# Products that nothing reads, in the lull slots of a TensorE plan

## The chip, the cores and the metric

The kernel runs on one core of a Trainium2 chip. The metric is device time in microseconds (us) of one launch. TensorE is called PE below, VectorE DVE, ScalarE ACT, GpSimd POOL, and SP issues most of the DMAs.

## The reference

The input is 32 images of 128 channels and 32 x 32 pixels. Four residual layers follow each other, each on a group-normalised copy of its input. The second one fills nearly all of the time.

```
x = x + conv3x3(gn(x))                       # layer 0
x = x + mamba_block(gn(x))                   # layer 1: 4 views of each image, 1024 steps each
x = x + coordinate_attention(gn(x)) * gn(x)  # layer 2: two short mambas over row and column means
x = x + quantum_circuit(gn(x))               # layer 3: a per-pixel map with 4 angles

# one mamba "way" (one view of one image), L = 1024, 256 inner channels, 16 states
h[t] = exp(dt[t] * A[n]) * h[t-1] + dt[t] * u[t] * B[t, n]
y[t] = sum over n of h[t] * C[t, n]  (+ D * u[t]),  then gated, projected, added
```

## The kernel before

**Tiling.** The 256 inner channels are two halves h of 128 partitions, and the 1024 pixels lie along the free axis. One *step* is one half and one state n: 32 steps make a way, four ways an image, and 32 images (and two short ways of the attention) give 4160 steps. `Steps.run` walks them.

**A step on the engines.** For step i ACT computes the decay `da` (L633). PE makes the input `bu` in PSUM (`spread`): in 11 of the 32 steps of a way ("turned" ones) by eight transposes of a tile that ACT has scaled (L647), in the other 21 by two bf16 products of 48 rows that copy B over the partitions (L653), after which DVE multiplies them by `du` in place (`input`, L669). DVE scans (`scan`, L677), POOL multiplies the scan's result `hh` by C (`weigh`, L686), and PE sums it over n into PSUM by eight transposes (`add`, `sum`, L722; for n = 0 there are eight products with the skip weights, L701, and the sum comes one iteration later). `bu` has two buffers, so PE may write step i + 1 when scan i - 1 has ended.

**The order.** Inside `manual_schedule` each engine executes in the order in which Python emits. One iteration i of `Steps.run` emits: the decay of step i + 3, reads of finished products (`flush`), `spread(i + 1)`, `scan(i)`, `input(i + 1)`, then one slot of the plan, `scale(i + 4)`, `weigh(i)`, `add(i - 2)` and the DMA that loads C for step i + 3.

**The plan.** All other work (convolutions, projections, dt, gates, statistics of the neighbouring images and ways) is cut into `Stage` objects with a hand-written cost for (PE, ACT, POOL, DVE). `Plan.slot` takes stages that are due, as long as each engine has credit; a slot is worth `SLOT = 3.3` us, and `load_of(i)` says what the step itself costs on the four engines. Since the streams have fixed windows relative to each way, the slots repeat from image to image: slot s of way q is filled alike in nearly all images. Some slots get no stage that uses PE.

**Products and their readers.** A stage takes one of two PSUM buffers of the pool `psm` by `Kernel.mm`; the instruction that reads it is kept in `waiting` (ACT), `behind` (DVE) or `single` (one half of a pair) and is emitted later by `flush`. `open` counts accumulations that are begun and not ended.

Of the kernel before, what the change touches and what calls it, by code (L numbers as in the profile page):

```python
# [12 lines left out]
F32 = mybir.dt.float32  # L13
# [6 lines left out]
P = 128  # L20
# [3 lines left out]
DS = 16  # L24
# [204 lines left out]
class Stage:  # L229


    def __init__(
        self, run, *, pe=0.0, act=0.0, pool=0.0, dve=0.0, takes=False, gap=1, at=0, when=lambda: True,
        pair=None,
    ):
        self.run, self.cost = run, (pe, act, pool, dve)


        self.takes, self.gap, self.at, self.when, self.pair = takes, gap, at, when, pair
# [257 lines left out]
class Plan:  # L497
# [16 lines left out]
    def slot(self, i, steps):  # L514

        k = self.k
        self.credit = [min(c + self.SLOT - own, self.SLOT) for c, own in zip(self.credit, steps)]

        def slack(s):
            return (s["end"] - i) / sum(stage.gap for stage in s["left"])  # L520

        for s in sorted((s for s in self.streams if s["start"] <= i), key=slack):
            stage = s["left"][0]
            if i < max(stage.at, s["last"] + stage.gap):
                continue
            if stage.takes and k.open > 1 or not stage.when():
                continue
            if stage.takes and self.pair not in (None, stage.pair) and slack(s) > 0.8:
                continue
            if slack(s) > 1.2 and any(c > 0 and c_ <= 0 for c, c_ in zip(stage.cost, self.credit)):  # L530
                continue
            stage.run()
            if stage.pair:
                self.pair = stage.pair if k.open or k.single else None
            self.credit = [c_ - c for c, c_ in zip(stage.cost, self.credit)]
            s["last"] = i
            s["left"].pop(0)
        late = [s for s in self.streams if s["left"] and s["end"] < i]
        assert not late, (i, [(s["start"], s["end"], len(s["left"])) for s in late])
        self.streams = [s for s in self.streams if s["left"]]  # L540

    def alone(self):

        k, i = self.k, 10**6
        while self.streams:
            for s in list(self.streams):
                k.flush(False)
                s["left"].pop(0).run()
                if not s["left"]:
                    self.streams.remove(s)  # L550
            k.flush(False)
        k.flush()


class Steps:
# [11 lines left out]
    def run(self, ways, plan):  # L567

        k = self.k
        steps = [(w, h, n) for w in ways for h in range(2) for n in range(DS)]  # L570
        self.steps = steps
        for i in range(3):
            self.load(i)
        for i in range(3):
            self.decay(i)
        self.spread(0)
        self.input(0)
        for i in range(len(steps) + 2):
            self.evict()
            self.decay(i + 3)  # L580
            k.flush(False, vector=False)
            self.spread(i + 1)
            self.catch_up()
            self.scan(i)
            k.flush(False)
            self.input(i + 1)
            if self.has(i):
                plan.slot(i, self.load_of(i))
            self.scale(i + 4)
            self.weigh(i)  # L590
            self.add(i - 2)
            self.load(i + 3)
        self.evict()
        k.flush()
# [123 lines left out]
    def sum(self, i):  # L718
        k, (w, h, n) = self.k, self.steps[i]
        t = self.hh.pop(i)  # L720
        for g, b, at in self.blocks(w):
            k.nc.tensor.matmul(  # L722
                self.y[g][: w.bl, b], t[:, at], k.ident,
                start=False, stop=(n == DS - 1 and b == w.per - 1), is_transpose=True,
            )
# [17 lines left out]
class Kernel:  # L743
# [21 lines left out]
    def exps(self):  # L765

        if not self.plain:
            self.nc.scalar.preload_act_table_set("natural_log_exp_and_others")  # L768
        self.plain = True

    def later(self, read, more=False, vector=False):

        if vector:
            self.behind.append(read)
        elif more:
            self.single = read
        else:
            self.waiting += [self.single, read] if self.single else [read]
            self.single = None
# [137 lines left out]
    def images(self):  # L917
        tc, nc, d = self.tc, self.nc, self.d
        with ExitStack() as ctx:
# [91 lines left out]
            def way_out(im, w):  # L1011


                def run(c):
                    def run():
                        cs = slice(c * 512, (c + 1) * 512)
                        if w.v == 0 and c == 0:
                            im.o = img.tile([P, HW], F32, tag="tmp", name="o")
                        ps = self.mm()
                        for h in range(2):  # L1020
                            nc.tensor.matmul(
                                ps, m.ow[:, w.v, h], w.sz[:, h, cs], start=(h == 0), stop=(h == 1)
                            )
                        into = im.o[:, cs]
                        had = into if w.v else im.hpad[:, 3 + c * 512 : 3 + (c + 1) * 512]
                        self.later(
                            lambda: nc.vector.scalar_tensor_tensor(
                                into, ps, 0.25, had, ALU.mult, ALU.add
                            ),
                            vector=True,  # L1030
                        )
                    return run

                return [Stage(run(c), pe=1.75, dve=0.7, takes=True, gap=2 - c) for c in range(2)]
# [513 lines left out]
```

## Time and profile before

| | us |
|---|---|
| median of 3 runs | 15073.83 (15066.03 to 15084.82) |
| profiled execution, its own time | 15093.06 |
| its span, first to last instruction | 15091.3 |
| mean granted TensorE clock | 0.920 of full speed |
| DVE busy | 13401.1 (89%) |
| PE busy | 13174.8 (87%) |
| POOL busy | 12747.8 (84%) |
| ACT busy | 12256.2 (81%) |

A busy PE is not a PE at its peak: its clock can be granted at half speed, and the same product then counts twice the time. What an engine waits for, and what ended the wait, stands behind each row of the groups, of the waits and of the timeline.

### The profile page before, as it was taken

How to read it: one execution, taken by the hardware profiler on the slowest of the kernel's cores; microseconds unless marked ns; L12 is line 12 of the kernel's file. 1: busy time of each engine (PE TensorE's matmuls, PEld its weight loads, DVE VectorE, ACT ScalarE, POOL GpSimd, SP SyncE). 2: the span in 40 equal slices, each digit the busy share in tenths (PEclk: the TensorE clock that was granted, in tenths of full speed). 3: DMA queues.
4: the chain of work that ended last, by engine and by line, in shares of the span. 5: the costliest groups of instructions: out<-in, count | busy, mean ns of one | idle time of the engine just before them, and what ended most of it. 6: DMA issues, size and time to landing. Idle time of an engine off the chain costs nothing. (4 is left out here: it accounts for less than half of the span.)

```text
span 15091.3 us, 197699 instructions
## 1 busy us (share of the span) xinstructions
PE 13174.8 (87%) x70318; PEld 8507.7 (56%) x70318; DVE 13401.1 (89%) x8776; ACT 12256.2 (81%) x21181; POOL 12747.8 (84%) x6529
## 2 busy tenths in 40 slices
PE   7888888888888888988888888888888888888876
PEld 4555555555555555555555555555555555555532
DVE  7999989999989999898999999999999999999774
ACT  6888888888888888888888888888888888888642
POOL 6888888888888888888888888888888888888764
PEclk8999999999999999999999999999999999999877
DMA  3444444444444444444444444444444444444431
GB/s 118 159 155 155 156 153 154 156 159 156 155 153 153 158 155 159 154 154 154 153 157 159 154 157 153 155 152 158 157 157 154 155 153 154 157 159 157 144 107 68
DMA packets 633895, 2277.61 MB, mean 151 GB/s; under 512 B 77481, under 2 KB 81145, under 8 KB 632777
## 3 DMA queue, kind: packets, MB, share of 16 engines
q1 hardware_dynamic: 630600, 2263.06, 43.8%
q8 instruction: 554, 9.08, 0.2%
q14 instruction: 437, 3.57, 0.1%
q10 hardware_dynamic: 2304, 1.90, 0.0%
HBM read 2221.35 MB, written 43.33 MB: 150 GB/s over the span
## 5 line engine op out<-in xcount | busy, mean ns | idle before, releaser
L686 POOL TENSOR_TENSOR hh<-hh,cc 128x1024 f32<-128x1024 f32 x4160 | 9771.8, 2366 | 1752.5 <-DVE hh L677 1086.5
L677 DVE TENSOR_TENSOR_SCAN hh<-da,bu 128x1024 f32<-128x1024 f32 x4160 | 9415.4, 2280 | 618.6 <-PE bu L647 234.9
L722 PEld LDWEIGHTS y<-cbig,hh 128*128 128x128 f32 x33280 | 4065.2, 150 | 1793.5 <-issue 1285.2
L722 PE MATMUL y<-cbig,hh 128*128 128x128 f32 x33280 | 4762.6, 290 | 181.8 <-POOL hh L686 181.4
L633 ACT ACTIVATE da<-dt,m_na 128x1024 f32<-128x1024 f32 x4096 | 4607.2, 1144 | 352.8 <-DVE hh L677 344.9
L669 DVE TENSOR_TENSOR bu<-du,bu 128x1024 f32<-128x1024 f32 x2752 | 3336.8, 1213 | 680.5 <-PE bu L653 679.6
L662 ACT ACTIVATE but<-dut,bt 128x128 f32<-128x128 f32 x11264 | 3433.6, 392 | 0.0
L653 PE MATMUL bu<-parts,sel 48*128 48x512 bf16 x5504 | 1761.5, 402 | 638.6 <-DVE hh L677 630.0
L280 PE MATMUL mm<-hpad,m_wc 128*128 128x512 f32 x4096 | 2063.6, 627 | 104.1 <-ACT relu L386 68.6
L647 PE MATMUL bu<-cbig,but 128*128 128x128 f32 x11264 | 1606.7, 290 | 378.1 <-DVE hh L677 331.6
L647 PEld LDWEIGHTS bu<-cbig,but 128*128 128x128 f32 x11264 | 1388.4, 151 | 445.2 <-issue 287.8
L280 PEld LDWEIGHTS mm<-hpad,m_wc 128*128 128x128 f32 x4096 | 710.1, 193 | 908.6 <-issue 753.5
L653 PEld LDWEIGHTS <-sel 48*128 48x128 bf16 x5504 | 322.6, 95 | 1149.9 <-DVE hh L677 687.2
L402 POOL TENSOR_TENSOR w<-w,du 128x1024 f32<-128x1024 f32 x260 | 613.8, 2361 | 38.3 <-ACT w L395 38.3
L299 PE MATMUL mm<-uc,m_xw 128*128 128x512 f32 x1024 | 602.9, 720 | 31.0 <-ACT sz L762 22.6
L701 PEld LDWEIGHTS y<-m_skip,uc 128*128 128x128 f32 x4096 | 554.4, 212 | 132.8 <-issue 79.8
L762 ACT ACT_TABLE_LOAD x483 | 619.7, 1283 | 8.5
L768 ACT ACT_TABLE_LOAD x483 | 619.7, 1283 | 8.5
L439 ACT COPY dut<-mm 128x512 f32<-128x512 f32 x512 | 294.9, 576 | 407.0 <-PE mm L434 406.9
L406 POOL TENSOR_TENSOR dt<-dt,w 128x1024 f32<-128x1024 f32 x260 | 615.3, 2366 | 0.2
L411 POOL TENSOR_TENSOR du<-dt,uc 128x1024 f32<-128x1024 f32 x260 | 614.3, 2363 | 0.2
L406 POOL TENSOR_TENSOR dt<-dt,relu 128x1024 f32<-128x1024 f32 x260 | 613.9, 2361 | 0.0
(219 smaller groups left out, 10394.3 us busy)
## 6 DMA issues: line engine op xcount, KB each, us to landing
cc<-rows SPq DMA_DIRECT2D x4160, 512.0 KB, 3.8
xt<-in_x SPq DMA_DIRECT2D x32, 512.0 KB, 5.9
x<-xt SPq DMA_DIRECT2D x32, 512.0 KB, 3.7
xt<-x SPq DMA_DIRECT2D x32, 512.0 KB, 4.0
out<-xt SPq DMA_DIRECT2D x32, 512.0 KB, 2.9
rows<-dbl SPq DMA_DIRECT2D x130, 64.0 KB, 4.3
stats<-st SPq DMA_DIRECT2D x32, 36.0 KB, 1.5
means<-stats SPq DMA_DIRECT2D x1, 1152.0 KB
```

The lines of the kernel that those rows point to most:

```text
L280: nc.tensor.matmul(self.view(ps), m.wc[:, v, j, h * P : (h + 1) * P], self.taps(j, c), start=(j == 0), stop=(j == 3),)
L406: nc.gpsimd.tensor_tensor(self.dt[h], self.dt[h], t[name], op)
L633: k.nc.scalar.activation(t, w.dt[h], AF.Exp, scale=w.m.na[:, h, n : n + 1])
L647: k.nc.tensor.matmul(t[:, b * P : (b + 1) * P], but[:, b], k.ident, start=True, stop=True, is_transpose=True,)
L653: k.nc.tensor.matmul(t[:, cs], k.sel[:, n], w.parts[:, cs], start=True, stop=True)
L662: k.nc.scalar.activation(t[:, b], w.dut[h][:, b], AF.Copy, scale=w.bt[:, b, n : n + 1])
L669: k.nc.vector.tensor_tensor(t, w.du[h], t, ALU.mult)
L677: k.nc.vector.tensor_tensor_scan(way(t), way(self.da.pop(i)), way(self.bu.pop(i)), 0.0, ALU.mult, ALU.add)
L686: k.nc.gpsimd.tensor_tensor(t, t, self.cc.pop(i), ALU.mult)
L722: k.nc.tensor.matmul(self.y[g][: w.bl, b], t[:, at], k.ident, start=False, stop=(n == DS - 1 and b == w.per - 1), is_transpose=True,)
L762: self.nc.scalar.activation(*args, AF.Silu, **kw)
L768: self.nc.scalar.preload_act_table_set("natural_log_exp_and_others")
```

## The change

`Plan.slot` now returns what is left of the slot by its own costs: SLOT, plus the DVE cost of the stages that it ran, less the PE cost of these stages and of the step. After `add(i - 2)`, `Steps.run` hands this, less 0.8 us, to a new function `Kernel.idle`. That one emits one product per 0.25 us, at most six, and none if there would be fewer than two or if more than one read is outstanding. The products have 48 rows and 512 columns in bf16 (the stationary operand is a piece of the identity, the moving one a piece of the selectors `sel`), all go into one tile `unread` from the pool `psm`, and nothing reads them. In the built program there are 2687 such products in 791 slots: 603 slots with three, 124 with six, 62 with two, two with five. Instructions of the other four engines stand in the same order as before.

```diff
@@ Plan.slot
         self.credit = [min(c + self.SLOT - own, self.SLOT) for c, own in zip(self.credit, steps)]
+        pe = dve = 0.0
...
             self.credit = [c_ - c for c, c_ in zip(stage.cost, self.credit)]
+            pe, dve = pe + stage.cost[0], dve + stage.cost[3]
...
         self.streams = [s for s in self.streams if s["left"]]
+
+        return self.SLOT + dve - pe - steps[0]
@@ Steps.run
-            if self.has(i):
-                plan.slot(i, self.load_of(i))
+            rest = plan.slot(i, self.load_of(i)) if self.has(i) else 0.0
             self.scale(i + 4)
             self.weigh(i)
             self.add(i - 2)
+            k.idle(rest - 0.8)
             self.load(i + 3)
@@ Kernel
+    def idle(self, us):
+
+        n = min(int(us / 0.25), 6)
+        if n < 2 or len(self.waiting) + len(self.behind) + self.open + bool(self.single) > 1:
+            return
+        ps = self.psm.tile([P, 512], F32, tag="mm", name="unread")
+        for _ in range(n):
+            self.nc.tensor.matmul(
+                ps, self.half[: 3 * DS], self.sel[:, :4].rearrange("p n d -> p (n d)"),
+                start=True, stop=True,
+            )
```

## The prediction

> **What bounds the kernel.** I read the page first: its busy row, its clock row, and in the groups what ended DVE's idle time.
>
> ```profile
> PE 13174.8 (87%) x70318; PEld 8507.7 (56%) x70318; DVE 13401.1 (89%) x8776; ACT 12256.2 (81%) x21181; POOL 12747.8 (84%) x6529
> ...
> PEclk8999999999999999999999999999999999999877
> ...
> L677 DVE TENSOR_TENSOR_SCAN hh<-da,bu 128x1024 f32<-128x1024 f32 x4160 | 9415.4, 2280 | 618.6 <-PE bu L647 234.9
> ...
> L669 DVE TENSOR_TENSOR bu<-du,bu 128x1024 f32<-128x1024 f32 x2752 | 3336.8, 1213 | 680.5 <-PE bu L653 679.6
> ```
>
> DVE sets the pace: no engine is busier, and what it waits for is PE, 680 us ahead of L669 and 235 us ahead of L677. These 915 us are all that faster products can win. PE is late for two reasons: heavy slots, and a clock that is now and then at half speed. The mean clock of 0.920 means that 2 x 0.080 x 15091 = 2415 us ran at half. The clock records show 417 such stretches, 2426 us together, most of them 3.41 us long. Between 200 and 14,400 us DVE idles 319 of 2017 us under a slow clock (15.8%), and 1000 of 12,183 us under a fast one (8.2%). If slow time cost what fast time does, 0.076 x 2017 = 153 us would be saved. That bounds the gain loosely from above.
>
> Then I cut a stretch of the second way of an image into 3.41 us windows at the clock's own edges (columns: window, its length, then PE, PEld, DVE, ACT, POOL busy, PEclk, DMA share, GB/s):
>
> ```profile
> 4646.14:4649.56 3.42, 1.49 (x11) 0.91 (x10) 3.29 (x3) 3.42 (x5) 2.42 (x2) 1.00 0.49 157
> 4649.56:4652.97 3.41, 2.88 (x10) 1.65 (x10) 3.38 (x5) 3.19 (x11) 3.38 (x2) 0.50 0.48 157
> ...
> 4690.52:4693.93 3.41, 2.63 (x11) 1.45 (x12) 3.28 (x3) 3.41 (x7) 2.56 (x2) 1.00 0.80 221
> 4693.93:4697.34 3.41, 3.41 (x12) 1.70 (x10) 2.64 (x2) 3.41 (x10) 2.81 (x2) 0.50 0.78 304
> 4697.34:4700.76 3.42, 3.42 (x13) 1.78 (x12) 2.71 (x2) 3.42 (x8) 1.88 (x1) 0.50 0.63 210
> 4700.76:4704.17 3.41, 3.41 (x17) 3.41 (x18) 3.38 (x6) 3.41 (x8) 2.37 (x1) 0.50 0.35 107
> 4704.17:4707.58 3.41, 2.27 (x18) 1.61 (x17) 3.41 (x2) 3.38 (x4) 1.17 (x1) 1.00 0.44 154
> 4707.58:4711.00 3.42, 2.54 (x22) 2.10 (x20) 2.94 (x3) 3.42 (x8) 3.42 (x2) 1.00 0.36 107
> ```
>
> Each window decides the clock of the next. A PE busy for 2.63 us loses it (4690.52), one busy for 2.27 us keeps it (4704.17). The difference is in the rows: the same windows for one line give 1.64 us of L377, products of 32 rows, in the first, and 1.50 us of L722, transposes of 128 rows, in the second. I sorted all 4414 windows by PE time at full clock (half of it while the clock is slow). Counting every product alike, the best threshold tells the next clock in 93% of them; counting a product by its rows over 128, a threshold of 1.35 us does in 96%.
>
> **What the Trainium skill says.** "TensorE: Matmul & The Clock Gate", Part 1, has a clock of two rates, set by activity in a free-running window of 3413 ns; the trace agrees (0.50 and 1.00 above, stretches of 3.41 and 10.24 us). Its Part 4 has transposes not count as busy in the same way; the trace disagrees, 4704.17 is kept by transposes. Its Part 2, "Back-to-back issue gap", prices 512 columns at 215.7 ns fast and 426.7 slow; the two products of L653 start 226 and 400 ns apart here, which I use. It has no word on rows.
>
> **The change, part by part.** Nothing is removed, and the order on the other four engines stays. PE gets 2687 products: 607 us at the fast price, 1075 us at the slow one. They stand after `add(i - 2)` and ahead of `spread(i + 2)`; so what is queued behind them is the `bu` for which DVE waits. I found the 791 places in this trace by counting L722 and L701. In 61% of the slots with three products and 83% of those with six, PE has no gap there as long as the products: the plan calls the slot empty, while PE still works off an earlier one. Only 274 of the 607 us fit into gaps.
>
> *Cost.* I carried each slot's extra time along PE until gaps took it up, and compared it at each `bu` with how early that `bu` was: 49 us if all products have the fast price, 110 us if those in slow stretches have the slow one. It falls on few places, which repeat in 31 images. The dearest is steps 15 and 16 of the second way, where three products come ahead of the L653 at 4699.71 and six ahead of the L647 at 4702.43:
>
> ```profile
> 4699.71 1.03 PE L653 MATMUL bu<-parts,sel 48*128 48x512 bf16 x2
> 4700.67 1.97 PE L722 MATMUL y<-cbig,hh 128*128 128x128 f32 x8
> 4702.43 1.89 PE L647 MATMUL bu<-cbig,but 128*128 128x128 f32 x8
> ...
> 4701.48 1.21 DVE L669 TENSOR_TENSOR bu<-du,bu 128x1024 f32<-128x1024 f32 x1
> ...
> 4704.03 4.42 DVE L677 TENSOR_TENSOR_SCAN hh<-da,bu 128x1024 f32<-128x1024 f32 x2
> ```
>
> PE is behind and slow. Three products (1.20 us) move the end of L653 from 4700.74 to 4701.94, so DVE's L669 starts 0.50 us later. L722 then ends its issue at 4703.63. The window up to 4704.17 now holds 0.88 us of L722 (1.76 at half), and by rows 0.18 of L653 and 0.13 of products: 1.19, under 1.35, where it had about 1.7 before (L722 and L647). So the clock stays slow for another window: six products take 2.40 us, L647 ends at 4707.92, and the second scan, which would start at 4706.77, starts at about 4708.05. Together 0.50 + 1.28 = 1.78 us an image, 55 us in 31. Were the clock fast again at 4704.17, L647 would end near 4706.3 and only the 0.50 would remain. The L647 of step 29 in ways three and four, behind three products, cost 38 us by the carried sum, all other places 24. Sum: 117 us.
>
> *Gain.* Where slow products delay DVE most, six products come ahead of 4649.52 and three ahead of 4654.23:
>
> ```profile
> 4655.19 3.78 PE L299 MATMUL mm<-uc,m_xw 128*128 128x512 f32 x4
> ...
> 4662.00 1.23 DVE L669 TENSOR_TENSOR bu<-du,bu 128x1024 f32<-128x1024 f32 x1 [0.64 <-PE bu L653]
> ...
> 4667.45 2.29 DVE L677 TENSOR_TENSOR_SCAN hh<-da,bu 128x1024 f32<-128x1024 f32 x1 [1.81 <-PE bu L647]
> ```
>
> L299 takes 3.78 us in place of 1.88, and DVE waits 0.64 + 1.81 = 2.45 us. The six products fit into a gap of 1.93 us. The window up to 4649.56 has 1.06 us by rows and gets 6 x 0.226 x 0.375 = 0.51: over 1.35, so the next is fast. That one then holds 0.86 of L722 and 0.375 x (0.43 of L653 + 0.68 of products) = 0.42: 1.28, just under. The clock falls again at 4652.97, ahead of L299, and DVE's wait stays. Other places gain little: steps 11, 15 of way one and 14, 15 of way four lose slow windows, but DVE waits for no product there. At step 9 of way three about 0.46 us an image may go, 14 us.
>
> *Waits.* A product waits for the last reader of its PSUM bank, and later tiles find the banks in another turn: 172 real tiles follow directly on another's bank that did not before. The skill's "PSUM — Partial Sum Buffer" (bank collisions) is why this needs a wait: two engines in one bank collide. In this trace these readers ended over 1.1 us ahead in all but two of the 172 places, and 786 of the 791 slots find theirs done. Bound: nothing to 10 us; I take 0.
>
> **Sum.** 117 - 14 = 103 us. DVE's later waits may swallow part, since PE's lateness has slack after them; I choose three quarters, 77 us. On the profiled execution's 15093 us that is 15170; the median lies 19 lower, so 15074 + 77, rounded to 15150.
>
> **Rivals.**
> *Faster (0.30).* A bf16 product of 48 rows counts like any other. Against: 32 and 48 rows fit better discounted. For: 96% isn't 100%, the weight is uncertain between 0.2 and 0.5, and the deciding window misses by 0.07 us; at 0.5 it passes. It decides at a weight of about 0.45. Then the window up to 4652.97 holds, L299 runs at 1.88 us, and 31 x 2.45 = 76 us go, with the 14; the products cost the fast price, 49. Net -41: 15033, and towards 15000 if more of the 153 us goes.
> *No change (0.15).* Both sums are about halved: the slow clock at 4704.17 ends as before, and delays are absorbed. 15074, within 30 us.
> *The banks (within slower).* If reads end later than in this trace, PE waits for ACT: up to 172 x 0.6 us = 103 us by a copy's 0.6 us, at most. Nothing speaks for it.
>
> **Numbers.** 0.2% (30 us) is about what a measurement of this kernel can tell from no change. Slower 0.55, same 0.15, faster 0.30. The likeliest case alone spans 15110 to 15200: 49 us less the gains absorbed at one end, no absorption and a second slow window at the other. With the faster case the range is 15000 to 15215.
>
> **What would show it.** Right: L782 about 230 ns a product when fast; mean clock at 0.93 or below; L299's slow 3.78 us still in the second way; the wait of L677 for L647 up by some 40 us, from step 16 of the second way. Wrong: a clock at 0.95, or the waits of L669 and L677 for PE down by 70 us. A new wait of L280, L377 or L434 on ACT would show the banks.

## The result and the profile after

The changed kernel takes 15303.73 us (median of 4 runs, 15300.38 to 15318.04). The kernel before, in the same comparison, takes 15076.3 us. The ratio is 1.0152, 95% interval 1.0139 to 1.0165: **slower by about 229 us**. The direction was forecast, with a third of the size (77 us); the time lies above the range, which ended at 15215. The profiled execution has a span of 15298.6 us, 207.3 us more than before.

The page after has these rows where the prediction quoted those of before (four lines were added above: L677, L669, L647, L653 and L722 of before are now L681, L673, L651, L657 and L726):

```profile
PE 13672.3 (89%) x73005; PEld 8535.2 (56%) x73005; DVE 13413.5 (88%) x8776; ACT 12266.3 (80%) x21181; POOL 12754.1 (83%) x6529
...
PEclk8999999999999999999999999999999999999877
...
L681 DVE TENSOR_TENSOR_SCAN hh<-da,bu 128x1024 f32<-128x1024 f32 x4160 | 9420.4, 2280 | 697.1 <-PE bu L651 276.1
...
L673 DVE TENSOR_TENSOR bu<-du,bu 128x1024 f32<-128x1024 f32 x2752 | 3337.4, 1213 | 788.4 <-PE bu L657 781.9
...
L782 PE MATMUL unread<-sel,half 48*128 48x512 bf16 x2687 | 796.9, 414 | 6.0 <-ACT relu L386 5.8
```

DVE has the same work (13,401 us before, 13,414 after) and waits longer for it: 276 + 782 = 1058 us for `bu`, where it was 915. That is 143 of the 207 us. A DVE operation still takes 1213 or 2280 ns (1213 and 2280 before), so what has grown is PE's lateness.

The second thing to see is what does not fit a simple story. The mean clock went *up*, from 0.920 to 0.935: 1998 us ran at half speed in place of 2426, in 291 stretches in place of 417. The kernel got slower with less slow time. So either the slow time that is left lies where it costs more, or PE is late for another reason. It also comes in longer pieces: 132 stretches of a single 3.41 us window are left of 226, and the mean stretch is 6.9 us, where it was 5.8.

**Where the time went.** For each step of each way I took the time from the end of the scan before it to the end of its own scan, averaged it over images 2 to 32, and subtracted before from after. The sum is 6.29 us an image, 195 us in 31; the first image adds 6.3 and the tail of the program 5.9 us. Together that is the 207.

| Place | us an image | us in 31 |
|---|---|---|
| way four, steps 28 to 31 | +1.97 | +61 |
| way three, steps 17 and 20 | +1.50 | +47 |
| way two, steps 15 to 18 | +1.34 | +42 |
| way three, steps 28 to 30 | +0.83 | +26 |
| way three, step 9 | -0.48 | -15 |
| all others together | +1.14 | +35 |

"All others" are not thin. They hold step 29 of way two with -1.85 and step 30 behind it with +2.49, together +0.64, steps 20 and 21 of way one with -0.79, step 26 of way one with +0.41 and step 9 of way two with +0.38; +0.50 is left for the other places.

The first row, in the trace. PE's timeline at this place in one image of the kernel before (columns: start, length, engine, line, operation, count, and the idle time ahead with what ended it):

```profile
4967.50 1.04 PE L647 MATMUL bu<-cbig,but 128*128 128x128 f32 x8
4969.73 1.09 PE L722 MATMUL y<-cbig,hh 128*128 128x128 f32 x8 [1.19 <-POOL hh L686]
4970.75 0.60 PE L653 MATMUL bu<-parts,sel 48*128 48x512 bf16 x2
...
4971.78 1.88 PE L280 MATMUL mm<-hpad,m_wc 128*128 128x512 f32 x4
```

and the same stretch of the same image after:

```profile
5034.19 1.09 PE L726 MATMUL y<-cbig,hh 128*128 128x128 f32 x8
5035.21 0.82 PE L782 MATMUL unread<-sel,half 48*128 48x512 bf16 x3
5035.96 1.09 PE L651 MATMUL bu<-cbig,but 128*128 128x128 f32 x8
5038.83 1.97 PE L726 MATMUL y<-cbig,hh 128*128 128x128 f32 x8 [1.78 <-POOL hh L690]
5040.73 1.03 PE L657 MATMUL bu<-parts,sel 48*128 48x512 bf16 x2
5041.69 1.11 PE L434 MATMUL mm<-cbig,du 128*128 128x128 f32 x4
5042.60 3.28 PE L280 MATMUL mm<-hpad,m_wc 128*128 128x512 f32 x4
```

Before, everything behind L647 runs at the fast clock: 0.60 us for L653, 1.88 for L280. After, the products stand ahead of L651, PE then waits 1.78 us for POOL, and all that follows has the slow clock: 1.03 us and 3.28. The windows of after at the clock's edges fit the prediction's rule (window, length, busy time of PE, PEld, DVE, ACT, POOL, PEclk, DMA share, GB/s):

```profile
5031.75:5035.16 3.41, 3.39 (x20) 1.85 (x19) 3.28 (x3) 3.41 (x8) 3.41 (x3) 1.00 0.45 155
5035.16:5038.57 3.41, 1.89 (x13) 1.07 (x11) 3.28 (x3) 3.41 (x9) 3.41 (x2) 1.00 0.38 157
5038.57:5041.99 3.42, 3.16 (x12) 2.00 (x13) 2.33 (x2) 3.39 (x4) 3.42 (x3) 0.50 0.48 153
5041.99:5045.40 3.41, 3.41 (x8) 1.85 (x7) 2.91 (x2) 3.41 (x5) 3.41 (x2) 0.50 0.70 228
```

The window that decides is the second. It holds the issue of L651 (eight in 0.87 us at the fast clock), a few hundredths of L726 and three products of 0.226 us. By rows that is 0.87 + 0.04 + 3 x 0.226 x 0.375 = 1.16 us, under the prediction's 1.35; had the products counted in full it would have been 1.59. The next two windows are slow. DVE pays for it:

```profile
5036.24 4.46 DVE L681 TENSOR_TENSOR_SCAN hh<-da,bu 128x1024 f32<-128x1024 f32 x2
5041.80 1.23 DVE L673 TENSOR_TENSOR bu<-du,bu 128x1024 f32<-128x1024 f32 x1 [1.09 <-PE bu L657]
```

L673 waits 1.09 us for the slow L657. Over the 31 images the share of slow time in step 29 of way four went from 0.09 to 0.75, in step 29 of way three from 0.02 to 0.61, in step 16 of way two from 0.07 to 0.50.

### The profile page after: what moved, and what is told of

Same layout as the page of the kernel before. It is cut to its first block, busy times and chain, and to the rows that moved or that the text cites. A ratio compares the mean times of both kernels' runs of the same rounds, so it can differ in the third digit from the quotient of the medians.

```text
span 15298.6 us, 203070 instructions
## 1 busy us (share of the span) xinstructions
PE 13672.3 (89%) x73005; PEld 8535.2 (56%) x73005; DVE 13413.5 (88%) x8776; ACT 12266.3 (80%) x21181; POOL 12754.1 (83%) x6529
## 5 line engine op out<-in xcount | busy, mean ns | idle before, releaser
L681 DVE TENSOR_TENSOR_SCAN hh<-da,bu 128x1024 f32<-128x1024 f32 x4160 | 9420.4, 2280 | 697.1 <-PE bu L651 276.1
L726 PEld LDWEIGHTS y<-cbig,hh 128*128 128x128 f32 x33280 | 3968.0, 147 | 1685.3 <-issue 1182.0
L726 PE MATMUL y<-cbig,hh 128*128 128x128 f32 x33280 | 4645.1, 286 | 144.3 <-POOL hh L690 143.8
L673 DVE TENSOR_TENSOR bu<-du,bu 128x1024 f32<-128x1024 f32 x2752 | 3337.4, 1213 | 788.4 <-PE bu L657 781.9
L657 PE MATMUL bu<-parts,sel 48*128 48x512 bf16 x5504 | 1731.6, 396 | 542.3 <-DVE hh L681 532.5
L280 PE MATMUL mm<-hpad,m_wc 128*128 128x512 f32 x4096 | 2037.2, 621 | 98.6 <-ACT relu L386 68.6
L651 PE MATMUL bu<-cbig,but 128*128 128x128 f32 x11264 | 1572.1, 285 | 160.7 <-DVE hh L681 104.7
L651 PEld LDWEIGHTS bu<-cbig,but 128*128 128x128 f32 x11264 | 1325.1, 147 | 416.8 <-issue 222.2
L280 PEld LDWEIGHTS mm<-hpad,m_wc 128*128 128x128 f32 x4096 | 707.3, 192 | 891.7 <-issue 747.2
L657 PEld LDWEIGHTS <-sel 48*128 48x128 bf16 x5504 | 341.0, 95 | 1090.2 <-DVE hh L681 593.0
L782 PE MATMUL unread<-sel,half 48*128 48x512 bf16 x2687 | 796.9, 414 | 6.0 <-ACT relu L386 5.8
L299 PE MATMUL mm<-uc,m_xw 128*128 128x512 f32 x1024 | 575.3, 690 | 47.0 <-ACT sz L766 38.5
```

The lines of the kernel that those rows point to most:

```text
L280: nc.tensor.matmul(self.view(ps), m.wc[:, v, j, h * P : (h + 1) * P], self.taps(j, c), start=(j == 0), stop=(j == 3),)
L651: k.nc.tensor.matmul(t[:, b * P : (b + 1) * P], but[:, b], k.ident, start=True, stop=True, is_transpose=True,)
L657: k.nc.tensor.matmul(t[:, cs], k.sel[:, n], w.parts[:, cs], start=True, stop=True)
L673: k.nc.vector.tensor_tensor(t, w.du[h], t, ALU.mult)
L681: k.nc.vector.tensor_tensor_scan(way(t), way(self.da.pop(i)), way(self.bu.pop(i)), 0.0, ALU.mult, ALU.add)
L726: k.nc.tensor.matmul(self.y[g][: w.bl, b], t[:, at], k.ident, start=False, stop=(n == DS - 1 and b == w.per - 1), is_transpose=True,)
```

## The experiments

My theory was: the products' own PE time costs little; the clock costs the rest, because a product of 48 rows counts for less than half in the window's activity while it uses a whole product's time, and so slow windows move into heavy work. The rivals: the PE time delays `bu` by itself; the turn of the PSUM banks adds waits; a few places make all of it. Clocks and waits below are those of the profiled execution, times are medians. Ratios were taken against runs of the kernel before in the same comparison, with medians from 15083.98 to 15084.64 us.

### Products of 128 rows in the same slots

```diff
-ps, self.half[: 3 * DS], self.sel[:, :4].rearrange("p n d -> p (n d)"),
+ps.rearrange("p (n d) -> p n d", d=P), self.half, self.half.unsqueeze(1).to_broadcast([P, 4, P]),
```

> As the changed kernel, the same slots and counts, but each product has 128 rows (identity times identity, 512 columns in bf16) in place of 48. Its time on TensorE is the same. Theory (the granted clock follows rows over 128; products of 48 rows fill slow windows without counting for them): the mean clock rises from 0.935 to 0.96 or more, and the time falls to 15000 to 15150 us. Rival 1 (only the products' own time on TensorE counts, the clock doesn't): 15304 us as the changed kernel, clock unchanged or the time unmoved by it. Rival 2 (waits for PSUM banks): 15304 us too.

Measured: 15027.27 us against 15083.98, ratio 0.996 (0.9945 to 0.9975). Same slots, same number of products, same columns; 277 us between this and the change. The clock is 0.953 (1421 us of slow time), where 0.96 or more was expected. In its groups (up to three releasers behind the idle time):

```profile
L681 DVE TENSOR_TENSOR_SCAN hh<-da,bu 128x1024 f32<-128x1024 f32 x4160 | 9413.6, 2280 | 577.7 <-PE bu L651 179.3 <-ACT da L637 24.0 <-POOL dt L406 6.9
...
L673 DVE TENSOR_TENSOR bu<-du,bu 128x1024 f32<-128x1024 f32 x2752 | 3335.4, 1212 | 638.3 <-PE bu L657 630.7
```

DVE's wait for `bu` is 810 us, below the 915 of before. PE does as many products ahead of the same `bu`, but the clock is not all that differs, as the expectation took it. In all these traces PE loses time where the number of rows changes from one product to the next. With the clock fast and no wait between, the last L726 starts 0.109 us ahead of a product of 128 rows and 0.205 us ahead of one of 48; three products and what stands around them, from the last L726 to the first L651, take 0.954 us with 48 rows and 0.757 with 128 (1.742 and 1.493 when slow). Where the products stand ahead of the 48-row L657 instead, the two kernels are alike (0.863 and 0.852). So 487 of the 791 slots are also shorter here by 0.20 us, 96 us in all at the fast clock, 121 at the slow one. That is the most that this PE time can make of the 277 us by itself; the split by places below bounds it closer.

### One small product a slot

```diff
-for _ in range(n):
+for _ in range(1):
...
+ps[:, :64], self.half[: 3 * DS], self.sel[:, 0, :64],
```

> As the changed kernel, but one product of 64 columns in each of the 791 slots, so the turn of the PSUM banks and every added wait stay, and nearly all added TensorE time goes[...]. Theory and rival 1: the time of the kernel before within 0.2% (15045 to 15105 us), clock 0.92. Rival 2 (banks): most of the 229 us stays, 15200 us or more.

Measured: 15073.49 us, ratio 0.9993 (0.9984 to 1.0001), clock 0.922. Every bank still has its new turn. The banks cost nothing, as I had taken it. The added PE time is not as small as expected: the rows still change from 128 to 48 and back, so a small product ahead of L651 takes 0.23 us of PE (0.205 + 0.130, less 0.109), and all 791 some 120 us at the fast clock. None of it shows in the kernel's time. It is as much as products of 48 rows take over those of 128 at the same 487 slots, which speaks against the change of rows as the cause of the loss.

### Only places with a gap, and only places without

The products repeat at the same steps in every image. `idle` was handed the place (way counted from 0, step), and a list of eleven places where PE had a gap in the trace of before decided (the comments are mine; the second run also keeps some 55 slots outside the 23 places that repeat):

```diff
+GAPS = {(0, 13), (0, 16), (0, 18), (1, 2), (1, 3), (1, 18), (2, 8), (2, 24), (3, 15), (3, 16), (3, 24)}
...
+if place not in self.GAPS:   # first run: only with a gap
+    return
...
+if place in self.GAPS:       # second run: only without
+    return
```

> The products of 48 rows only in the 11 places of an image where TensorE had a gap of about their length in the trace of the kernel before (ahead of steps 13, 16, 18 of way one, 2, 3, 18 of way two, 8, 24 of way three, 15, 16, 24 of way four), none in the other 12. Theory: the loss came from the places without a gap; 15030 to 15090 us, at most a small gain since the clock rises little (0.93). If the places with a gap take part in the loss (a slow stretch only moved to a worse place): above 15130 us.

> The products of 48 rows only in the 12 places of an image where TensorE had no gap in the trace of the kernel before, none in the other 11. Theory (the whole loss comes from these places): 15290 to 15380 us, the changed kernel's 15304 plus the 20 to 30 us that the places with a gap gained. Rival 1 (the two sets only do harm together, for instance since the first moves slow stretches ahead of the second): 15100 to 15200 us.

Measured, at 48 rows: with a gap 15055.34 us, ratio 0.999 (0.9982 to 0.9998); without a gap 15378.62, ratio 1.0199 (1.0184 to 1.0214). The places without a gap lose 294 us, more than the whole change. The eleven with one gain about 15 us alone (29 by the medians), and some 70 us when they are added to the others. The clock of the second is 0.914, below that of before. That fits the theory: where PE has no gap, a product of few rows takes the place of real ones in the window and thins it out.

### The same split with 128 rows

> The same 12 places, products of 128 rows: the same TensorE time, but rows that count for the clock. Theory: what is left is the products' own time at the fast price, 15080 to 15140 us; the difference to the run with 48 rows (150 us or more) is the clock's part of the loss. If the products' time were the larger part: 15200 us or more.

> The 11 places with a gap alone, and products of 128 rows. With 48 rows there: 0.999 of the kernel before. With 128 rows in all 23 places: 0.996. Theory: the slow stretch of steps 1 to 3 of way two goes and no product delays a bu: 14940 to 15030 us, ahead of both. Rival: the harmful places help the clock too when their products have 128 rows, and the gaps alone give 15040 to 15080 us.

Measured: without a gap 15046.34 us, 0.9975 (0.9965 to 0.9986), clock 0.938; with a gap 15076.35, 0.9993 (0.9984 to 1.0002), clock 0.942. The first turns a loss of 294 us into a gain of 38, beyond the expectation (15080 to 15140). The change of rows can make 58 us of these 332 at the most: 234 of the slots stand ahead of L651, and each would count with its 0.25 us at the slow clock. The rest, over 270 us, is left to the clock, whose slow time is 1880 us in place of 2649. This is the run that tells the clock from the PE time.

The second missed the expectation of my theory (14940 to 15030) and fell into the rival's 15040 to 15080. Yet the slow stretch that the theory aimed at did go: L299 of way two takes 1.98 us in place of 3.78, and steps 4 and 5 behind it are 1.33 us an image shorter. Part came back elsewhere: +0.66 at step 8 of way two, +0.82 at its steps 29 and 30, +0.30 at step 17 of way three. This profiled execution is the fastest of the twelve; 1.42 us an image are left in it, in the median 8 us in all. Less slow time at one place moves delays to others, and the mean clock does not show it.

### Without the four places that the prediction named dearest

```diff
+GAPS = {(1, 15), (1, 16), (2, 29), (3, 29)}
...
+if place in self.GAPS:
+    return
```

> The changed kernel without the products in four of its 23 places of an image: ahead of steps 15 and 16 of way two and ahead of step 29 of ways three and four, where the prediction put 93 of its 117 us. By the steps' times in the changed kernel these sites lost 1.3, 0.8 and 2.0 us an image, 133 us in 32: 15304 - 133 = 15170 us, and with the steps of way three that follow from nothing visible (1.5 us an image at steps 17 and 20) left over. If the loss only moves to the next slow stretch: 15250 us or more.

> Products of 128 rows, left out ahead of steps 15 and 16 of way two and of step 29 of ways three and four. With 48 rows this placing gave 1.0051 of before, and all 23 places with 128 rows 0.996. Theory by the carried sum: the four places cost at most 30 us at the fast price, so 14990 to 15030 us. If the products there help the clock more than they delay, as in the 12 places without a gap: above 15030 us.

Measured: at 48 rows 15160.59 us, 1.0051 (1.0036 to 1.0066), clock 0.939: without these four places 143 of the 229 us are gone (152 by the ratios). At 128 rows 15030.85 us, 0.9966 (0.9957 to 0.9974), on the line between the theory and its rival: leaving them out changes nothing against 15027.27. So the places that the prediction picked carry most of the loss, and products of 128 rows cost nothing there. Some of the loss only moves: without the four, steps 9 and 14 of way two are 1.67 us an image longer than before, where the change has 0.38, and steps 17 and 20 of way three keep 1.41 of their 1.50.

### Products of 16 rows

```diff
+ps, self.half[:16], self.sel[:16, :4].rearrange("p n d -> p (n d)"),
```

> The changed kernel with products of 16 rows in place of 48, in all 791 slots; their time is the same. Theory: with a weight of 16/128 they fill slow windows and count even less: clock below 0.935, slower than the changed kernel, 15320 to 15420 us. Rival (a threshold in what a product is, for instance fp32 or bf16, not its rows): 15304 us as the changed kernel.

Measured: 15447.37 us, 1.0248 (1.0222 to 1.0275), clock 0.911, 2757 us of slow time in stretches of 8.5 us on average. Fewer rows, more loss, a little above the expectation. Some of it is PE time: ahead of the 48-row L657, 300 slots now have one more change of rows (0.954 us in place of 0.863), 27 to 40 us of the 144 in all. In its groups:

```profile
L681 DVE TENSOR_TENSOR_SCAN hh<-da,bu 128x1024 f32<-128x1024 f32 x4160 | 9423.2, 2280 | 775.7 <-PE bu L651 347.7 <-ACT da L637 38.8 <-POOL hh L690 12.6
...
L673 DVE TENSOR_TENSOR bu<-du,bu 128x1024 f32<-128x1024 f32 x2752 | 3338.4, 1213 | 886.0 <-PE bu L657 883.5
...
L782 PE MATMUL unread<-sel,half 16*128 16x512 bf16 x2687 | 859.5, 439 | 0.8 <-ACT relu L386 0.6
```

DVE's wait for `bu` is 1231 us. With the others that makes a series of the same slots and columns (with 128 rows both operands come from the identity):

| Rows of a product | us | clock | DVE's wait for `bu` |
|---|---|---|---|
| 16 | 15447 | 0.911 | 1231 |
| 48 | 15304 | 0.935 | 1058 |
| 128 | 15027 | 0.953 | 810 |
| (no products) | 15076 | 0.920 | 915 |

### Rows without products: the real `spread` padded to 128

If rows are what counts, no product has to be added. This kernel is the one before, with the 48 rows of `parts` and `sel` padded to 128 by rows of zeros, so that the existing product of L653 reads 128 rows (the lines are shortened; `parts` had two buffers before, too):

```diff
+np.concatenate([s, np.zeros((P - 3 * DS, DS, P), np.float32)])
...
+self.sel = cst.tile([P, DS, P], BF16, name="sel")
...
+self.parts = k.parts[k.turn % 2]      # two fixed tiles, zeroed once
+k.later(lambda: nc.scalar.copy(self.parts[: 3 * DS], ps[: 3 * DS]))
```

> The kernel before, without any added product: only the two products that spread B over the partitions (L653, 48 rows in 21 of 32 steps) take 128 rows, of which 80 are zero in both operands. TensorE's time, the order and the result stay. Theory (rows count for the clock): each such step has 0.45 us of TensorE time that counts whole in place of 48/128, so slow windows go without any new delay: mean clock 0.95 or more, 14900 to 15030 us. Rival (rows don't matter; what matters is what the added products displace): clock 0.92, the time of the kernel before within 0.2%.

Measured: **14800.59 us** against 15084.23, ratio 0.9815 (0.9801 to 0.983), clock 0.955. This beats both kernels, and the expectation (14900 to 15030). In its groups (the wait of PE for DVE, in the third row, is the mirror image):

```profile
L679 DVE TENSOR_TENSOR_SCAN hh<-da,bu 128x1024 f32<-128x1024 f32 x4160 | 9400.7, 2279 | 504.5 <-PE bu L649 134.1 <-ACT da L635 8.3 <-POOL da L638 6.5
...
L671 DVE TENSOR_TENSOR bu<-du,bu 128x1024 f32<-128x1024 f32 x2752 | 3331.3, 1211 | 462.4 <-PE bu L655 462.2
...
L655 PE MATMUL bu<-parts,sel 128*128 128x512 bf16 x5504 | 1715.9, 395 | 878.3 <-DVE hh L679 877.7
```

DVE's wait for `bu` falls from 915 to 596 us, and PE waits 878 us for DVE where it was 630. The added rows are zeros in both operands, and PE is busy for less time (12,228 us; 13,175 before), yet the clock is higher: what counts for it is neither the values nor the busy time alone.

But the time has a second cause that this run does not keep apart. A product takes no longer (395 ns, 402 before), and the changes of rows around it are gone. The same place of one image at the fast clock, before and padded:

```profile
4975.24 1.04 PE L722 MATMUL y<-cbig,hh 128*128 128x128 f32 x8
4976.21 0.60 PE L653 MATMUL bu<-parts,sel 48*128 48x512 bf16 x2
4976.74 0.70 PE L280 MATMUL mm<-hpad,m_wc 128*128 128x512 f32 x1
...
4870.02 1.04 PE L724 MATMUL y<-cbig,hh 128*128 128x128 f32 x8
4870.90 0.59 PE L655 MATMUL bu<-parts,sel 128*128 128x512 bf16 x2
4871.33 1.02 PE L281 MATMUL mm<-hpad,m_wc 128*128 128x512 f32 x2
```

From L722 to L280 it is 1.50 us before and 1.31 padded: 0.10 us less ahead of the two products and 0.10 behind them. In 2752 steps this frees some 500 us of PE. How much of the 283 us is the clock and how much this time stays open. The run with 128 rows in the added products has nearly the same slow time (1421 us; 1338 here) and takes 227 us more; that speaks for the freed time, though that run also carries the products.

### Both

> The changed kernel with 128 rows both in the spreading products and in the ones that nothing reads. Theory: clock 0.97 or more; if the slow windows that are left were worth more than the products' own time, below both the run with 128 rows in the products (0.996 of before) and the one with 128 rows in the spread, 14850 to 14980 us; if not, between them.

Measured: 14808.95 us, 0.9819 (0.9803 to 0.9836), clock 0.975, 735 us of slow time. The time lies level with the padded kernel's, where the expectation had it below or between. Products of 128 rows on top take another 605 us of slow time away and win nothing: DVE's wait for `bu` is 605 us, 596 without them. Whether that slow time cost nothing, or the products' own time took the gain back, was not separated.

## Why the prediction was right or wrong

- **The bound, right.** DVE's wait for PE's `bu` moves with the time: 1231, 1058, 915, 810 and 596 us in kernels of 15447, 15304, 15076, 15027 and 14801.
- **The rule by rows, right, with the sign that follows from it.** It was read off the windows of before (96% against 93%), with a weight between 0.2 and 0.5 left open. The runs with 128 rows in the same slots, above all those without a gap, settle that rows count; the rival in which 48 rows count like 128 is out. Sorted in a like way (a product is busy until it ends or the next one starts), the windows of the other traces agree: by rows the next clock is told in 95% before, 96% after, 97% with 16 rows and 98% in the padded kernel, counting alike in 91, 91, 89 and 97%. The best threshold lies between 1.4 and 1.6 us there, not at 1.35, so a margin of 0.07 us was finer than the rule.
- **The gain, right.** Step 9 of way three gave 0.48 us an image (0.46 forecast). In way two L299 keeps its slow 3.78 us: step 2 is slow for 0.97 of its time, as the window of 1.28 us said, though by that thin margin.
- **Way two, right.** Steps 15 to 18 cost 1.34 us an image (1.78 forecast); the share of slow time in step 16 is 0.50, and 11 of 31 images have the extra slow window.
- **The cost, mis-sized: the step that failed.** *Step 29 of ways three and four* was put at 38 us, from PE's carried lateness alone; around it the kernel lost 26 + 61 = 87. There the prediction carried the delay along PE, but did not redo the window as it had for step 16 of way two: it kept the slow windows of before where they were, and priced the products by them. In the changed kernel the window with the products falls short, and the slow window comes on L726, L657 and L280. All *four dear places* were put at 93 us, and leaving them out saves 143 to 152. *All other places*, 24 us less the gain of 14, make 76 to 86. Of these, steps 17 and 20 of way three alone cost 47. The window does not explain them: no products stand within eight steps ahead of step 17 (its slow share rises from 0.02 to 0.23), and step 20 loses 0.44 of its 0.53 us with products of 128 rows, too. Their cause stays open.
- **The price of a product, too low in 487 slots.** The products start 216 ns apart when fast and 426 when slow (226 and 400 were taken). The change of rows, which was priced at nothing, adds more: three products ahead of L651 take 0.85 us of PE when fast and 1.53 when slow, not 0.68 and 1.20. Both changes at a slot have to be paid there, since L651 has 128 rows; ahead of L657, which has 48, three products take 0.66 us, as priced.
- **The factor of three quarters, wrong.** It was a choice with no figure behind it. Without it the sum is 103 us, still half of the 207.
- **The slack ahead, wrong in kind.** A fast clock was taken to be worth something by total slow time ("153 us bound the gain"). With 428 us less slow time the kernel lost 207 us. Where the slow time lies decides, and a mean does not show it. That padding won 283 us does not refute the bound: it also freed PE time.
- **The signs to look for.** The wait of L681 for L651 is up by 41 us (40 forecast), and that is luck: step 16 of way two has 19 of it, step 29 of ways three and four 32 and 26, step 31 of way four 24, and step 29 of way two took 66 off. The wait of L673 for L657 is up by 102, which the text did not have; 75 of it are at step 30 of way two. The clock was to be 0.93 or below: 0.935. No new wait on ACT for a bank appeared.

What stays open: whether activity is in proportion to rows or goes in steps of some rows (only 16, 48 and 128 were run; 64 and 96 would tell); what moves the delays at steps 17 and 20 of way three and at steps 29 and 30 of way two; and how the gain of the padded kernel divides between the clock and the freed PE time.

## What to carry to other kernels

A filler product keeps TensorE's clock only if it counts, and where PE has no gap a filler that counts for little lowers the clock. So before adding work, look at the rows of the work that is there: padding a 48-row product to 128 with zeros made no product longer, took the changes of rows out of PE's stream, raised the clock and took 1.85% off this kernel. Price an added product from the start of the one ahead of it to the start of the one behind it, not from the product alone. And place a slow window before pricing it: ask which `bu` is due in the window after, and carry the window forward at every place, not at the dearest one only.

## What the runs showed of the hardware

The size of the effect of rows on the clock was not expected. With the same number of products, of the same columns, in the same slots, the slow time was 2757 us (16 rows), 1998 (48) and 1421 (128), and the kernel's time 15447, 15304 and 15027 us, a part of which is PE time for changes of rows. Rows of zeros count like any others: with 80 of 128 rows zero, in weights and data, the mean clock rose from 0.920 to 0.955, while PE was busy for less time.

A change in the number of rows between neighbours costs PE time. Behind a transpose of 128 rows a product of 128 rows starts after 0.109 us and one of 48 after 0.205; behind a product of 48 rows and 512 columns a 128-row one starts after 0.306 us, behind one of 128 rows after 0.216 (all at the fast clock, medians of the kernel before and of the padded one).

And a higher mean clock does not go with a shorter time: 0.935 was slower by 1.5% than 0.920.
